# A four-layer graph network on one core: seven-product gates and one operation list that treats the SBUF way shared by VectorE and GpSimd as held by one engine at a time

## Chip, cores, metric

One NeuronCore of a Trainium2 chip; everything is fp32. The metric is the device time of one execution in microseconds.

## The reference, cut to what matters

128 graphs of 64 nodes with 256 features go through four residual layers, each behind a layer norm and a relu. Two graphs share the 128 partitions, and four such pairs form a group, so there are 16 groups of 512 nodes.

```python
h = relu(layernorm(x)); x = x + gat(h, adj, ...)      # layer 0: attention, 4 heads of 64
h = relu(layernorm(x)); x = x + gat(h, adj, ...)      # layer 1: attention, 1 head of 256
h = relu(layernorm(x)); x = x + relational(h, ...)    # layer 2: with 0/1 edges only its loop direction counts
h = relu(layernorm(x))                                # layer 3: gated recurrence, 3 steps
for i in range(3):
    m = h @ weight[i]; aggr = A.T @ m
    gi = aggr @ w_ih.T + b_ih; gh = h @ w_hh.T + b_hh
    r = sigmoid(i_r + h_r); z = sigmoid(i_z + h_z); n = tanh(i_n + r * h_n)
    h = (1 - z) * n + z * h
x = x + h
```

## The kernel before

Three stages stand one behind the other: attention (two groups alternating, layer 0 of one beside layer 1 of the one before), the relational layer, the recurrence. The recurrence of one step, with features on partitions (`c` is the half of the features, a `gate` is four matmuls of 512 columns for r and z and two for each part of n):

```python
into, own = (wc[:, i], aT), (whh, hT)
hnew = work.tile([P, K, T], F32, name="hT")
for c in range(K):
    pr = gate("rz", c, (own, into))
    ph = gate("nn", 4 + c, (own,))
    pi = gate("nn", 4 + c, (into,))
    pz = gate("rz", 2 + c, (own, into))
    nc.scalar.activation(r, pr, AF.Sigmoid, bias=brz[:, c : c + 1])
    nc.vector.scalar_tensor_tensor(t, ph, bh[:, 4 + c : 5 + c], r, op0=ALU.add, op1=ALU.mult)
    nc.vector.tensor_tensor(t, t, pi, ALU.add)
    nc.scalar.activation(nt, t, AF.Tanh, bias=bi[:, 4 + c : 5 + c])
    nc.scalar.activation(z, pz, AF.Sigmoid, bias=brz[:, 2 + c : 3 + c])
    nc.gpsimd.tensor_tensor(d, hT[:, c, :], nt, ALU.subtract)
    nc.gpsimd.tensor_tensor(d, d, z, ALU.mult)
    nc.vector.tensor_tensor(hnew[:, c, :], nt, d, ALU.add)
# ... cut: hnew back to nodes on partitions by 8 transposes
```

## Time and profile before

| | before |
|---|---|
| time, median of the first 3 runs | 2235.72 us (2230.89 to 2236.61) |
| TensorE busy, granted clock | 83%, 0.879 |
| VectorE / ScalarE / GpSimd busy | 46% / 20% / 19% |

Busy shares are averages over stages with different limits, so the prediction reads the span in slices and stretches. It shows those lines.

### The profile page before, as it was taken

What the parts mean: (1) busy time and instruction counts of PE and PEld (TensorE: products, weight loads), DVE (VectorE), ACT (ScalarE), POOL (GpSimd) and SP (SyncE); (2) the same over time, 40 slices, a digit from 0 to 9 for tenths busy, and PEclk for the clock granted to TensorE, in tenths of its full rate; (3) what the DMA queues carried; (4) which work ended last, traced back from release to release, by engine and by line L of the source; (5) the groups of instructions that cost most, each with busy time, mean ns of one, the idle gap of its engine ahead of it and who ended that gap; (6) DMA issues with size and microseconds to landing.
All of it is one profiled execution on the core that took longest, in us unless ns stands there. A gap on an engine that the chain in (4) does not pass through costs nothing.

```text
span 2234.7 us, 16784 instructions
## 1 busy us (share of the span) xinstructions
PE 1865.9 (83%) x6149; PEld 1072.5 (48%) x6149; DVE 1019.7 (46%) x2244; ACT 442.4 (20%) x708; POOL 432.6 (19%) x364
## 2 busy tenths in 40 slices
PE   3857675766666668887999999999999999999998
PEld 2545454555455434444444544544444454444444
DVE  4576767676767554433433323332333233333222
ACT  1122222122222112222111111121112111111111
POOL 1111221122112210000222122222212212121221
PEclk8876666666666579998999999999999999999999
DMA  8000000000000000000000000000000000000000
GB/s 230 29 1 0 1 0 0 1 1 0 0 0 1 0 2 0 1 0 0 1 10 10 10 0 10 10 10 0 10 10 10 0 10 10 10 3 8 10 10 10
DMA packets 31592, 23.95 MB, mean 11 GB/s; under 512 B 11280, under 2 KB 31504, under 8 KB 31504
## 3 DMA queue, kind: packets, MB, share of 16 engines
q1 hardware_dynamic: 25344, 18.88, 2.7%
q10 hardware_dynamic: 6160, 3.94, 0.6%
q8 instruction: 50, 0.82, 0.1%
q14 instruction: 38, 0.31, 0.0%
HBM read 14.43 MB, written 8.39 MB: 10 GB/s over the span
## 4 chain that ended last, share of the span: by engine, by line
PE 73%; DVE 15%; ACT 6%; POOL 4%; issue 2%; DMA 1%; POOLq 0%; ACTq 0%; DVEq 0%
PE rz L535 27%; PE nn L535 14%; PE mm L289 6%; PE mm L468 5%; PE mm L228 4%; PE tp L524 4%; PE tp L284 3%; POOL d L556 3%; PE tp L154 2%; PE ht L568 2%; PE mm L491 2%; PE pe L248 2%; DVE em L301 2%; DVE var L143 2%; ACT eb L273 2%
## 5 line engine op out<-in xcount | busy, mean ns | idle before, releaser
L535 PE MATMUL rz<-hT,whh 128*128 128x512 f32 x768 | 378.1, 596 | 4.7 <-ACT hT L155 4.7
L535 PE MATMUL rz<-aT,wc 128*128 128x512 f32 x768 | 366.1, 599 | 0.0
L555 POOL TENSOR_TENSOR d<-hT,nt 128x512 f32<-128x512 f32 x96 | 121.5, 1266 | 740.8 <-ACT nt L551 740.8
L557 DVE TENSOR_TENSOR hT<-nt,d 128x512 f32<-128x512 f32 x96 | 66.4, 692 | 434.5 <-POOL d L556 434.5
L535 PEld LDWEIGHTS rz<-aT,wc 128*128 128x128 f32 x768 | 139.6, 190 | 173.1 <-issue 144.7
L535 PEld LDWEIGHTS rz<-hT,whh 128*128 128x128 f32 x768 | 138.3, 191 | 142.7 <-issue 134.5
L535 PE MATMUL nn<-hT,whh 128*128 128x512 f32 x384 | 185.7, 592 | 0.0
L284 PE MATMUL tp<-ident,eb 128*128 128x128 f32 x320 | 80.8, 416 | 121.4 <-ACT eb L273 121.4
L535 PE MATMUL nn<-aT,wc 128*128 128x512 f32 x384 | 180.4, 592 | 0.0
L546 ACT ACTIVATE r<-rz,brz 128x512 f32<-128x512 f32 x96 | 66.0, 687 | 517.9 <-PE rz L535 517.9
L289 PE MATMUL mm<-wh,ec 128*128 128x65 f32 (+1 forms) x640 | 160.9, 423 | 3.8 <-DVE ec L285 2.4
L548 DVE SCALAR_TENSOR_TENSOR t<-nn,bh,r 128x512 f32<-128x512 f32 x96 | 72.0, 750 | 201.0 <-PE nn L535 172.1
L154 PE MATMUL tp<-ident,hn 128*128 128x128 f32 x512 | 94.6, 337 | 75.6 <-DVE hn L147 70.5
L289 PEld LDWEIGHTS mm<-wh,ec 128*128 128x128 f32 x640 | 136.8, 302 | 26.6 <-DVE ec L285 18.3
L556 POOL TENSOR_TENSOR d<-d,z 128x512 f32<-128x512 f32 x96 | 121.4, 1264 | 105.6 <-ACT z L553 105.6
L468 PE MATMUL mm<-hT,wl 128*128 128x512 f32 x256 | 120.5, 614 | 17.6 <-ACT sg L473 13.8
L155 ACT ACTIVATE hT<-tp 128x512 f32<-128x512 f32 x128 | 71.2, 594 | 299.2 <-PE tp L154 289.6
L284 PEld LDWEIGHTS tp<-ident,eb 128*128 128x128 f32 x320 | 65.5, 236 | 129.3 <-ACT eb L273 129.3
L228 PE MATMUL mm<-w0e,hT 128*128 128x264 f32 x256 | 81.0, 454 | 55.6 <-DVE es L233 54.6
L551 ACT ACTIVATE nt<-t,bi 128x512 f32<-128x512 f32 x96 | 69.3, 721 | 279.2 <-DVE t L549 279.2
L154 PEld LDWEIGHTS tp<-ident,hn 128*128 128x128 f32 x512 | 78.2, 175 | 94.9 <-DVE hn L147 82.2
L535 PEld LDWEIGHTS nn<-aT,wc 128*128 128x128 f32 x384 | 73.0, 190 | 91.8 <-issue 91.8
(95 smaller groups left out, 2210.0 us busy)
## 6 DMA issues: line engine op xcount, KB each, us to landing
X<-in_x_dram SPq DMA_DIRECT2D x16, 512.0 KB, 6.5
out_dram<-hnat SPq DMA_DIRECT2D x16, 512.0 KB, 2.9
A<-in_adj_dram SPq DMA_DIRECT2D x16, 128.0 KB, 6.0
ihn<-in_L_gnn_w_ih_dram ACTq DMA_DIRECT2D x1, 768.0 KB, 10.8
wn<-in_L_gnn_weight_dram ACTq DMA_DIRECT2D x3, 256.0 KB, 2.6
ihn<-in_L_gnn_w_hh_dram ACTq DMA_DIRECT2D x1, 768.0 KB, 4.8
w0e<-in_L_gnn_W_dram ACTq DMA_DIRECT2D x1, 256.0 KB, 4.4
w1e<-in_L_gnn_W_dram ACTq DMA_DIRECT2D x1, 256.0 KB, 5.8
```

Of the source, the lines that this page charges most:

```text
L154: nc.tensor.transpose(pt[:, p * P : (p + 1) * P], hn[:, p, k * P : (k + 1) * P], ident)
L155: nc.scalar.activation(hT[:, k, :], pt, AF.Relu)
L228: nc.tensor.matmul(pm[:, : D + 2 * heads], hT[:, k, p * P : (p + 1) * P], we[:, k, :], start=(k == 0), stop=(k == K - 1),)
L284: nc.tensor.transpose(pt[:, h * P : (h + 1) * P], eb[:, first + h, :], ident)
L289: nc.tensor.matmul(pv[:, h, :], ec[:, p * heads + h - first, :], wv[:, p, h, :], start=True, stop=True)
L468: nc.tensor.matmul(pm, wl[:, k, col : col + P], hT[:, k, :], start=(k == 0), stop=(k == K - 1))
L524: nc.tensor.matmul(pa[:, p * P : (p + 1) * P], hnat[:, p, c * P : (c + 1) * P], abd[:, p, :], start=True, stop=True,)
L535: nc.tensor.matmul(pg, l, r, start=(j == 0), stop=(j == len(ops) - 1))
L548: nc.vector.scalar_tensor_tensor(t, ph, bh[:, 4 + c : 5 + c], r, op0=ALU.add, op1=ALU.mult)
L551: nc.scalar.activation(nt, t, AF.Tanh, bias=bi[:, 4 + c : 5 + c])
L555: nc.gpsimd.tensor_tensor(d, hT[:, c, :], nt, ALU.subtract)
L556: nc.gpsimd.tensor_tensor(d, d, z, ALU.mult)
```

## The change

The intent: fewer columns through TensorE for the r and z gates, no stage that leaves TensorE waiting, and an order of each engine's instructions that is worked out in advance. The program is first recorded as operations with their dependencies, a duration, and a deadline by group and layer. A list maker then issues them to the engines' queues by an own clock: of what could start earliest, the one due first.

The 1696 lines of the diff come to four pieces. First the clock, with the shared way: the access to SBUF that VectorE and GpSimd cannot use at the same time (the prediction shows it in a trace). `port` is how long an operation needs it:

```diff
+            t, _, op, places = best          # key = (start, due), over all engines
+                # ... cut: the operation is issued; DMA queue apart
+                took = op.cost
+                if op.port:
+                    other = "Pool" if e == "DVE" else "DVE"
+                    took = max(took, held[other] + min(op.port, took) - t)
+                    held[e] = t + took
+# ... cut
+def port(engine, method, writes, reads):
+    if method not in ("tensor_tensor", "scalar_tensor_tensor", "tensor_scalar", "tensor_copy"):
+        return 0.0
+    n = elements(writes[0])
+    reads = [v for v in reads if elements(v) >= n]
+    if engine == "gpsimd":
+        return 50.0 + 2.1 * n if n >= 64 else 0.0
+    if engine != "vector" or any(v.base.pool.psum for v in [*writes, *reads]):
+        return 0.0
+    return 15.0 + n * (1.04 if len(reads) > 1 else 0.53)
```

Then the seven products. The halves of the nodes `S0`, `S1`, the halves of the features and the two gates r and z make a product of two 2x2 block matrices; sums of the blocks (`ws` of weights, `ms` of states, made on GpSimd) let seven products of 256 columns do for eight. The partial results are read from PSUM by copies and additions in between:

```diff
-                    pr = gate("rz", c, (own, into))
-                    pz = gate("rz", 2 + c, (own, into))
+                # ... cut: one product is a pair of weights and states, chosen by its number
+                    1: (w[:, 0, cs], m[:, 0, S0]),
+                    2: (w[:, 1, cs], m[:, 1, S0]),
+                    3: (ws[:, 2, cs], m[:, 1, S1]),
+                    4: (w[:, 1, zs], ms[:, 3]),
+                    5: (ws[:, 0, cs], ms[:, 0]),
+                    6: (ws[:, 1, cs], ms[:, 1]),
+                    7: (w[:, 0, zs], ms[:, 2]),
```

Third, attention builds its weights as min(max(t·g, f), mask) of exponentials, with sources on the free axis: no transposes of the weights, no maximum to subtract. Fourth, sigmoids become tanh of half the argument, and the features are fetched per group instead of staying on chip. The general relational path moved behind a flag test at the end and does not run on this data.

The deadlines are constants of the program, in us: `start, period = 100, 91.8`, times of the layers for the first three groups, and for later groups `end - 70 * i` with `end = start + g * period - 49`.

## The prediction

> **What bounds the kernel now.** I read the page's table by engine and its 40 slices first, then busy time in four stretches cut where the stages change, then the chain of waits inside two of them, then the groups by line.
>
> ```profile
> PE   3857675766666668887999999999999999999998
> DVE  4576767676767554433433323332333233333222
> PEclk8876666666666579998999999999999999999999
> ```
>
> Two kernels stand one behind the other here. In the first half neither TensorE nor VectorE is full and the granted clock is at 0.6 to 0.7. In the second half TensorE is full at full clock while VectorE falls to a third. The stretches give numbers:
>
> ```profile
> core 0: us, PE busy (x) PEld busy (x) DVE busy (x) ACT busy (x) POOL busy (x), PEclk, DMA share, GB/s
> 0.00:55.00 55.00, 17.17 (x44) 10.56 (x45) 25.00 (x71) 5.96 (x9) 8.29 (x13) 0.89 0.83 234
> 55.00:850.00 795.00, 532.47 (x1985) 400.13 (x1985) 520.53 (x1241) 168.13 (x296) 155.30 (x132) 0.69 0.01 3
> 850.00:1085.00 235.00, 191.50 (x638) 104.93 (x637) 98.90 (x276) 55.54 (x91) 20.14 (x20) 0.95 0.00 0
> 1085.00:2234.00 1149.00, 1124.76 (x3488) 556.92 (x3487) 375.31 (x656) 212.76 (x312) 248.91 (x199) 1.00 0.02 8
> ```
>
> Attention (55 to about 805 us) is bound by a chain that passes from engine to engine; the recurrence (from 1054 us) is bound by TensorE. The chain in each:
>
> ```profile
> 424.33 1.24 DVE t L253
> 425.58 1.22 DVE t L259
> 426.81 0.33 DVE t L253
> 427.14 1.25 DVE t L262
> ```
> ```profile
> 1505.15 6.01 PE rz L535 x14
> 1511.15 3.43 PE nn L535 x8
> ```
>
> In attention the end hangs on VectorE steps of 1.2 us in a row, with TensorE standing. In the recurrence it is matmul after matmul: 14 passes in 6.01 us, 429 ns each. So the GRU stage can only become shorter by fewer columns through TensorE, and the attention stage only by putting it beside something else.
>
> **The columns, before.** An fp32 matmul is two passes in this trace, a transpose one. Start to start of neighbours in the trace: 429 ns at 512 columns, 222 at 264, 217 at 258, 216 at 256, 109 to 112 at 128 and 112 at 65 (the fastest tenth at full clock). By the counts of the groups by line: r and z gates 1536 x 0.429 = 659 us; n gates 768 x 0.429 = 329; values of the two attention layers 256 x 0.222 + 256 x 0.217 = 112; loop weights 256 x 0.429 = 110; everything else (transposes, 65-column aggregates, adjacency products, weights) 401. Sum **1611 us**, of a span of 2235. The other 624 us are idle time and half clock, nearly all before 1085 us.
>
> **What the Trainium skill says.** "TensorE: Matmul & The Clock Gate", Part 1: after an idle window of about 3.4 us the array's clock falls to half, and sustained work brings it back. This trace agrees: 0.69 in attention, 1.00 in the recurrence. "Perfetto Trace Analysis", Optimization Strategy: where the most contended engine changes over time, interleave those regimes; this trace is such a case, and this is what the change does. "SBUF — State Buffer", Who interferes with whom: VectorE in a two-port mode, or with two SBUF inputs, and a GpSimd operation that reads SBUF exclude each other for the whole instruction. The trace agrees at least for the one-input kind:
>
> ```profile
> 409.74 2.34 POOL L304 TENSOR_TENSOR X<-X,em 128x1024 f32<-128x1024 f32 x1 [3.20 <-DVE em L303]
> ```
> ```profile
> 409.85 2.25 DVE L143 TENSOR_SCALAR var<-mv 128x4 f32<-128x4 f32 x1
> ```
>
> A VectorE operation on four elements, 170 ns at the median, takes 2.25 us and ends as GpSimd's addition ends. The two-input kind never meets GpSimd in this kernel, so no run shows it yet. "ScalarE: Activation LUTs", Table sets: exp and tanh are in one set. Before loads tables four times (1.28 us each); after replaces sigmoid by tanh of half the argument and has one load. Worth 4 us, no more.
>
> **Part 1, seven products instead of eight.** For r and z the two halves of the features, the two gates and the two halves of the nodes make a 2x2 by 2x2 product. It is done with seven products of 256 columns where eight halves stood. The order of the changed kernel has 1344 such matmuls: 2688 passes x 0.216 = 581 us against 659. Saved on TensorE: **78 us**. Added: four sums per state or aggregate, 384 on GpSimd, each 185 + 2.11 x 256 = 725 ns (the line through its 1266 ns at 512 and 2347 ns at 1024 elements); one copy on ScalarE and one addition on VectorE for three of the four half gates.
>
> **Part 2, attention without its matrices turned.** The weights are built with sources already on the free axis, so the 320 transposes of eb (35 us), most of the pe products (34 us) and 128 transposes of vT (14 us) go; small transposes and the early groups' products come in (11 us). Saved: **72 us**. The subtraction of the maximum, the predicated copy and the reduction per head on VectorE go as well. New is a way through DRAM for one row per group and head, which has tens of us to land in, as it is listed a period ahead.
>
> The TensorE floor after: 581 + 329 + 112 + 110 + 329 for everything else = **1461 us**.
>
> **Part 3, one list for everything.** Group g's recurrence runs beside the attention and loop layers of later groups, each engine's order fixed in advance with durations that match this trace (427 ns a pass, 682 ns for a 512-element VectorE operation, 1275 for GpSimd). So the 624 us should shrink to: a head, a tail, and what TensorE still waits.
> Head: the first matmul started at 23.1 us here, behind the input; the first groups' layers are one dependent chain, and by 55 us TensorE had done 17 us of work. Halving the first groups helps a little. I take 45 us of idle.
> Tail: the last recurrence has no filler left. Its three layers wait for a chain of aT copy (0.59), three sums on GpSimd (2.2) and, at the end, addition, tanh, two VectorE steps on a half (0.4 each): about 5 us a layer, 15 us, plus output (2.9 us to land). I take 20 us.
> Middle: the old recurrence kept TensorE busy 1124.76 of 1149 us, 98%, with coarse pieces. Now TensorE has 1611 waits listed (1484 before) in pieces of half the size, with fuller engines beside it. I choose **95%**: 1461 / 0.95 = 1538.
> Sum: 45 + 20 + 1538 = 1603, say **1600 us**, a ratio of 0.716.
>
> **The other engines, by the same rows.** VectorE: layernorms 227 us (unchanged); recurrence 192 x 5 + 96 = 1056 operations on 256 elements at 0.40 (the busy time per instruction of o) = 420; attention about 300, loop 100, the rest 55. Sum 1100 us, 69% of 1600. ScalarE: 288 copies at 0.37, 576 tanh at 0.415 (the 64x256 row), 96 biases at 0.69, 160 copies of 512 at 0.59, and the layers' own, about 735 us, 46%. GpSimd: 576 x 0.725 = 418, powers 70 x 1.01 = 71, additions to x 28 x 2.35 = 66, others 20: 575 us, 36%. The shared way: GpSimd's 555 us of reading plus VectorE's two-input and two-port operations (recurrence 576 x 0.41 = 236, attention 171, others about 75) make some 1040 us held, 65%. It fits. Unplanned, about 1000 such VectorE operations would meet GpSimd with chance 555/1600 and lose some 0.45 us: 160 us, which brings VectorE to 79%. The list counts this, so I expect less.
>
> **The rivals.**
> 1. VectorE with the shared way becomes the bound. If every microsecond of GpSimd blocked VectorE: 1100 + 555 = 1655, with head and tail about 1720. For it: 2.25 us for four elements, as shown, and nearly every new VectorE operation of the recurrence has two SBUF inputs. Against: VectorE reads PSUM or one input in a good half of its time, and the order is made for this.
> 2. The recurrence's own chain becomes the bound. 48 layers in 1500 us leave 31 us each; TensorE's own work in one is (581 + 329 + 85 + 42) / 48 = 21.6 us, so about 10 us of filler must land in the right gaps. If the chain needs 34 us a layer: 48 x 34 + 100 before the first = 1730. For it: seven products add copies and sums to the chain, and a fixed order cannot swap in what is ready. Against: the old chain of gate, tanh and state cost 2.9 us per layer and was hidden to 98%.
> 3. The list holds almost exactly: 98% and a head and tail of 55 us give 1491 + 55 = 1546. For it: the period written into the plan, 91.8 us, is 3% over 1461 less the 29 us of setup, by 16 groups (89.5). I do not take more from that number than intent.
> 4. The clock does not come up, because short waits still leave idle windows. At 0.9 instead of 1.0, 1461 becomes 1623 and the total about 1760. Against: the recurrence held 1.00 over 1149 us, and even at 81% busy (850 to 1085 us) the clock was 0.95.
>
> **Range and chances.** Rival 3 sets the lower end, 1550; a middle of 91% with head and tail of 70 us sets the upper, 1461 / 0.91 + 70 = 1675, which I draw in to 1665, since rivals 1 and 2 each have perhaps one chance in ten. Slower than before by 2% would need 2280 us, hundreds above the worst rival; only the general branch being taken, which the data's 0/1 edges exclude, could do it. Faster 0.98, same 0.01, slower 0.01.
>
> **What would show it.** In the profile after: TensorE at full clock and 9 in nearly every slice from about 60 us on; its busy share over 90%; matmul steps of 216 ns in the ry, rm and rz products; VectorE between 65% and 80%, and GpSimd near 36%, evenly over the span; the chain that ended last mostly TensorE. Step 1 is wrong if the 256-column passes follow each other at more than 230 ns (weight loads no longer hidden). Step 3 is wrong if a stretch in the middle shows TensorE under 90%; the waits of TensorE then name the rival: VectorE operations of z, d or hT lasting far over 0.41 us for rival 1, sums on GpSimd or aT on ScalarE for rival 2, a clock under 0.97 for rival 4. The whole is wrong if the span is under 1530 or over 1700.

## The result

| | before | after |
|---|---|---|
| time, median of 4 runs each | 2233.3 us | 1551.68 us (1549.9 to 1553.41) |
| ratio | | 0.6947 (0.6933 to 0.6961) |
| TensorE busy, granted clock | 83%, 0.879 | 96%, 0.988 |
| VectorE / ScalarE / GpSimd busy, us | 1020 / 442 / 433 | 1152 / 717 / 641 |

Predicted were 1600 us and a range of 1550 to 1665. The result lies just inside its lower end.

The same three rows of the page as before, 40 slices of the changed kernel's span:

```profile
PE   5979999999999999999999999999999999999997
DVE  6778786968688686878868697886969778666444
PEclk8979999999999999999999999999999999999999
```

The two regimes of before are gone. From the fourth slice to the last but one TensorE is at 9 at full clock, and VectorE is at 6 to 9 until the last three slices, where it is at 4. The dip in the third slice belongs to the head of the program. In stretches (busy time of each engine, granted clock, DMA share, GB/s):

```profile
core 0: us, PE busy (x) PEld busy (x) DVE busy (x) ACT busy (x) POOL busy (x), PEclk, DMA share, GB/s
0.00:60.00 60.00, 40.12 (x168) 29.03 (x169) 39.70 (x122) 20.12 (x57) 20.43 (x37) 0.91 0.47 132
60.00:120.00 60.00, 50.33 (x205) 33.85 (x203) 43.91 (x139) 21.15 (x57) 16.34 (x25) 0.83 0.04 10
120.00:1400.00 1280.00, 1267.04 (x5878) 944.50 (x5877) 993.13 (x2543) 609.89 (x1388) 555.08 (x620) 1.00 0.07 20
```

In the changed kernel every operation passes through one recording helper, so all lines are L370 and the tiles tell the groups apart: `hn` normalised features, `eb` attention weights, `aT` aggregate, `hT` state, `aS` and `hS` their sums, `r` and `z` gates, `t` candidate, `d` difference of state and candidate. TensorE's longest waits there (who waited, for whom, us in total, times, longest):

```profile
PE tp L370 <- DVE hn L370: 14.3, 1, 14.3
PE rm L370 <- DVE hT L370: 8.8, 13, 0.9
PE tp L370 <- DVE var L370: 6.1, 1, 6.1
PE mm L370 <- DVE eb L370: 5.0, 5, 2.3
```

14.3 us are the wait for the first input and 6.1 us a single wait at 101 us; the wait that repeats most is for the state `hT`, as a next step's first products start.

**Where the 682 us went.** Passes start one after another at 429 ns for 512 columns, 216 for 256 and 109 to 112 for 128 in the changed kernel too, seven products included. So I can weigh all passes at those times, as the prediction did ("floor"), and call the rest of a stretch lost:

| | floor | lost |
|---|---|---|
| before, whole span 2234.7 | 1611 | 623 |
| after, whole span 1551.6 | 1461 | 91 |
| after, 0 to 120 us | 71.8 | 48.2 |
| after, 120 to 1400 us | 1253.5 | 26.5 |
| after, 1400 to 1551.6 us | 135.6 | 16.0 |

By this account 150 us of the gain are fewer columns, 532 us are time that TensorE no longer loses to waits and half clock.

**The shared way.** GpSimd's and VectorE's timelines of the changed kernel at 631 us (start, duration):

```profile
631.19 2.35 POOL L370 TENSOR_TENSOR xg<-xg,hn 128x1024 f32<-128x1024 f32 x1 [3.81 <-DVE hn L370]
```
```profile
632.02 1.80 DVE L370 SCALAR_TENSOR_TENSOR t<-r,t 128x256 f32<-128x256 f32 x1 [0.39 <-ACT r L370]
```

An operation with two SBUF inputs that takes 0.42 us alone begins inside GpSimd's addition, takes 1.80 us and ends 0.28 us after it. The groups by line show who suffers (count, busy us, mean ns of one):

```profile
L370 DVE SCALAR_TENSOR_TENSOR t<-r,t 128x256 f32<-128x256 f32 x192 | 128.6, 675 | 97.6 <-ACT r L370 74.6 <-ACT t L370 21.1
L370 DVE SCALAR_TENSOR_TENSOR hT<-d,t 128x256 f32<-128x256 f32 x192 | 102.8, 553 | 2.4
L370 DVE SCALAR_TENSOR_TENSOR d<-z,d 128x256 f32<-128x256 f32 x192 | 100.7, 536 | 38.1 <-POOL d L370 22.6 <-ACT z L370 14.9
L370 DVE TENSOR_TENSOR z<-rz,z 128x256 f32<-128x256 f32 x192 | 80.4, 419 | 68.5 <-PE rz L370 57.5 <-ACT z L370 10.1
```

The same number of elements four times: `z` has one input in PSUM and takes 419 ns whether GpSimd works or not (418 and 419 ns in the trace); `t`, `hT` and `d` have both in SBUF and take 416 to 418 ns without GpSimd beside them, and 960, 717 and 661 ns on average with it. Over all VectorE operations I count about 155 us lost so, and 71 us on GpSimd (time beyond each form's undisturbed duration).

### The profile page after: what moved, and what is told of

Its sections match the earlier page's. It is cut to its first block, busy times and chain, and to the rows that moved or that the text cites. A ratio compares the mean times of both kernels' runs of the same rounds, so it can differ in the third digit from the quotient of the medians.

```text
span 1551.6 us, 20462 instructions
## 1 busy us (share of the span) xinstructions
PE 1496.4 (96%) x6837; PEld 1106.9 (71%) x6837; DVE 1152.0 (74%) x2971; ACT 716.9 (46%) x1645; POOL 641.1 (41%) x748
## 4 chain that ended last, share of the span: by engine, by line
PE 79%; DVE 12%; POOL 4%; issue 2%; ACT 2%; DMA 1%; ACTq 0%; SPq 0%; DVEq 0%
PE mm L370 20%; PE ry L370 18%; PE nh L370 10%; PE tp L370 9%; PE ni L370 8%; PE rz L370 8%; PE rm L370 5%; DVE hT L370 3%; POOL aS L370 2%; DVE d L370 2%; DVE hn L370 2%; DVE t L370 2%; POOL hS L370 1%; DVE eb L370 1%; POOL d L370 1%
## 5 line engine op out<-in xcount | busy, mean ns | idle before, releaser
L370 POOL TENSOR_TENSOR d<-hT,t 128x256 f32<-128x256 f32 x192 | 149.7, 790 | 460.8 <-ACT t L370 459.5
L370 DVE SCALAR_TENSOR_TENSOR t<-r,t 128x256 f32<-128x256 f32 x192 | 128.6, 675 | 97.6 <-ACT r L370 74.6
L370 PE MATMUL nh<-hT,whh 128*128 128x512 f32 x384 | 195.4, 597 | 1.8 <-DVE hT L370 1.8
L370 PE MATMUL ni<-aT,wc 128*128 128x512 f32 x384 | 194.3, 594 | 0.0
L370 ACT ACTIVATE z<-z,brz 128x256 f32<-128x256 f32 x192 | 97.1, 506 | 75.2 <-DVE z L370 75.0
L370 DVE TENSOR_TENSOR z<-rz,z 128x256 f32<-128x256 f32 x192 | 80.4, 419 | 68.5 <-PE rz L370 57.5
L370 DVE SCALAR_TENSOR_TENSOR d<-z,d 128x256 f32<-128x256 f32 x192 | 100.7, 536 | 38.1 <-POOL d L370 22.6
L370 POOL TENSOR_TENSOR hS<-hT 128x256 f32<-128x256 f32 x96 | 81.1, 849 | 105.1 <-PE ry L370 94.8
L370 PE MATMUL mm<-wl,hT 128*128 128x512 f32 x248 | 121.0, 598 | 0.0
L370 ACT COPY z<-ry 128x256 f32<-128x256 f32 x192 | 71.0, 370 | 107.7 <-PE ry L370 88.3
L370 POOL TENSOR_TENSOR aS<-aT 128x256 f32<-128x256 f32 x96 | 92.2, 961 | 58.8 <-ACT aT L370 58.8
L370 DVE TENSOR_SCALAR hn<-xg,mv,rstd 128x256 f32<-128x256 f32 x256 | 115.1, 491 | 1.4 <-POOL rstd L370 1.2
L370 PE MATMUL ry<-hS,wsum 128*128 128x256 f32 x384 | 115.3, 382 | 0.4 <-ACT z L370 0.4
L370 PE MATMUL rz<-hS,whh 128*128 128x256 f32 x384 | 114.9, 381 | 0.5 <-DVE z L370 0.5
L370 PE MATMUL ry<-aS,wsum 128*128 128x256 f32 x384 | 114.3, 379 | 0.0
L370 PE MATMUL rz<-aS,wc 128*128 128x256 f32 x384 | 114.2, 379 | 0.0
L370 POOL TENSOR_TENSOR rstd<-var,mhalf 128x4 f32<-128x4 f32 (+1 forms) x70 | 74.5, 1069 | 95.2 <-DVE var L370 93.8
L370 PE MATMUL tp<-abd,hnat 128*128 128x128 f32 x768 | 108.6, 276 | 0.0
L370 PEld LDWEIGHTS tp<-abd,hnat 128*128 128x128 f32 x768 | 103.0, 192 | 5.9 <-issue 1.4
L370 PEld LDWEIGHTS ry<-hS,wsum 128*128 128x128 f32 x384 | 69.6, 190 | 51.7 <-issue 24.3
L370 PE MATMUL tp<-ident,hn 128*128 128x128 f32 x512 | 85.7, 278 | 20.9 <-DVE hn L370 14.3
L370 POOL TENSOR_TENSOR aS<-aT,aS 128x256 f32<-128x256 f32 x96 | 88.7, 925 | 41.5 <-ACT aT L370 40.7
```

The lines of the kernel that those rows point to most:

```text
L370: return do(*[real(a) for a in args], **{k: real(v) for k, v in kwargs.items()})
```

## The experiments

Twelve kernels ran, all correct. Times are medians; "lost" is as above. Comparisons go over ratios to the kernel before, as the chips differ: its median was 2230 to 2236 us throughout.

| run | us | ratio | TensorE's share at floor, 120 to 1400 us |
|---|---|---|---|
| after | 1551.7 | 0.6947 | 97.9% |
| e1 shared way not counted | 1636.9 | 0.7334 | 91.4% |
| e2 eight products | 1601.3 | 0.7176 | 99.5% |
| e3 program order | 3137.0 | one look | 47.9% |
| e4 more columns | 1616.5 | 0.7246 | 99.4% |
| e5 longer, not exclusive | 1590.9 | 0.7118 | 95.3% |
| e6 eight products, sums kept | 1606.1 | 0.7184 | 99.2% |
| e7 other deadlines | 1525.6 | 0.6825 | 99.4% |
| e8 those, way not counted | 1565.9 | 0.7003 | 96.4% |
| e9 eight products, e7's deadlines | 1598.8 | 0.7160 | 99.8% |
| e10 more columns, e7's deadlines | 1609.1 | 0.7207 | 99.4% |
| e11 subtraction on VectorE | 1519.7 | 0.6805 | 99.4% |
| e12 order by deadline | 2669.1 | one look | 53.2% |

### e1: the shared way not counted

```diff
 def port(engine, method, writes, reads):
+    return 0.0
```

> Only the list changes: its clock no longer holds VectorE back while GpSimd has the shared way, or the other way round. The instructions are the same, so TensorE's floor stays 1461 us. Theory (the counting is worth time, because a listed order cannot swap in what is ready): VectorE's two-input operations on 256 elements (t, d, hT) lengthen beyond the 675, 536 and 553 ns of the changed kernel, TensorE falls from 98% to 95% or 96% between 200 and 1400 us, and the span is 1580 to 1620 us. Rival (VectorE at 74% has slack enough, the semaphores absorb it): span within 0.7% of 1552 us, 1541 to 1562, whatever the operations last.

1636.86 us, ratio 0.7334: 85 us more than the changed kernel for the same instructions in another order. The direction is the theory's, beyond its numbers. But its means of getting there failed. The groups by line of e1:

```profile
L370 DVE SCALAR_TENSOR_TENSOR hT<-d,t 128x256 f32<-128x256 f32 x192 | 109.5, 582 | 4.1
L370 DVE SCALAR_TENSOR_TENSOR t<-r,t 128x256 f32<-128x256 f32 x192 | 104.8, 546 | 88.7 <-ACT r L370 68.9 <-ACT t L370 19.1
L370 DVE SCALAR_TENSOR_TENSOR d<-z,d 128x256 f32<-128x256 f32 x192 | 99.5, 530 | 39.6 <-POOL d L370 24.1 <-ACT z L370 15.1
```

`t` is shorter than in the changed kernel (546 against 675 ns), `hT` a little longer, `d` the same. Over all of VectorE about 138 us are lost to the way, against 155. The list that counts the way does not avoid collisions; VectorE loses a little more time in them. What it does is expect them. TensorE's longest waits in e1:

```profile
PE tp L370 <- DVE hT L370: 20.7, 16, 2.6
PE tp L370 <- DVE hn L370: 14.2, 1, 14.2
PE mm L370 <- ACT aT L370: 12.7, 13, 1.1
PE tp L370 <- DVE var L370: 6.7, 2, 6.3
PE ry L370 <- ACT z L370: 6.5, 14, 0.5
PE mm L370 <- DVE o L370: 6.2, 23, 0.7
```

In place of one repeated wait there are many, on VectorE and on ScalarE. I read them so: the list placed matmuls at moments at which their operands would have been ready, had VectorE not been held, and as the order is fixed, nothing else could be taken in their place. The waits fit this reading; they do not prove it, and e5 and e8 test it further.

### e2: eight products

The chunk's products 1 to 7, their copies and additions and all sums are replaced by:

```diff
+            def prod(self, name, k, source):
+                w, m = ((whh, self.hT), (wc[:, self.i], aT))[source]
+                f = {"rm": 0, "rz": D}[name] + self.c * P
+                ps, new = self.bank(name)
+                nc.tensor.matmul(ps, w[:, k, f : f + P], m[:, k, :], start=new, stop=(source == 1 and k == 1))
```

> The r and z gates as before, eight half products (768 matmuls of 512 columns), without the sums of weights and states, the copies and the additions; the freed PSUM bank goes to the shared pool. Same list maker. Theory (TensorE's columns bind): floor 1461 + 78 = 1539 us and about the same 90 us lost, so 1620 to 1640 us. Rival (what the seven products add on GpSimd, 384 sums of about 0.87 us, on ScalarE, 288 copies, and on VectorE, 288 additions, costs time too, so taking it away gives part back): 1575 to 1610 us.

1601.34 us, ratio 0.7176: 50 us more than with seven products, where TensorE's floor grows by 78 (1461 to 1539). The rival's range held, though not its reason, as e6 and e9 show. The 28 us between them lie mostly in the middle of the span: eight products lost 6.6 us from 120 to 1400 us, seven 26.5. What eats them stays open here; e6, e7 and e9 take it up.

### e3 and e12: the same operations in plainer orders

e3 takes operations as the program states them, e12 by deadline, both without the clock:

```diff
-                        key = (t, op.due)
+                        key = (op.number, 0)          # e3;  (op.due, op.number) in e12
```

> Same operations, but each engine's list is the order in which the program states them, group after group, without any look at time. Theory (the list's interleaving, not the cheaper attention, makes most of the gain): a group's three layers (a chain of some 85 us) and its recurrence (69 us of columns and its own waits) follow each other, 16 x 150 to 190 us = 2400 to 3000 us, TensorE clock under 0.8. Rival (fewer operations and columns do most, and engines that run ahead through their queues do the rest): under 1800 us.

> Same operations and same deadlines as the changed kernel, but the list takes, of all operations whose inputs are listed, the one due first; it has no clock and does not ask when an engine is free or an operand there. Theory (interleaving by deadlines alone is not enough; each engine must be given what will be ready when it is free): 2100 to 2500 us, between e3 and the changed kernel. Rival (any interleaved order fills TensorE): under 1750 us.

3137.03 and 2669.14 us, one look each, both slower than the kernel before and beyond the top of the range expected, with the cheaper attention and the seven products in place. The page of e3, then that of e12:

```profile
PE   5584664847557375574746648466583755738466
PEclk8696786968869587786967868678696876958778
```
```profile
PE   6654657777777668767776776767667676867776
PEclk8775778888888889868798888789888878879888
```

TensorE is at 3 to 8 with the clock at 0.5 to 0.9 from end to end. Even an order that interleaves groups by deadline (e12) leaves it waiting: its longest wait, 262.5 us in all, is for VectorE's `hT` before the state is transposed, and the fixed order lets nothing be taken in between.

### e4: more columns for TensorE alone

```diff
+                if name == "nh" and new:
+                    nc.tensor.matmul(ps, w[:, k, f : f + P], m[:, k, :], start=True, stop=True)
                 nc.tensor.matmul(ps, w[:, k, f : f + P], m[:, k, :], start=new, stop=not new)
```

> The first matmul of each nh gate is issued twice (the second begins the sum anew, so the result is the same): 96 x 2 passes of 429 ns = 82 us more on TensorE and nothing on any other engine. Theory (TensorE binds over nearly the whole span): 1552 + 82 = 1634 us, at least 1620. Rival (another engine or the chain of the recurrence binds, and TensorE has room): below 1585 us.

1616.5 us, ratio 0.7246: 65 us for 82 us of columns. That is near the theory, but short of its least number by 3.5 us. In the middle TensorE loses 8 us now, not 26.5: the added columns took the place of some waits, or the list, made anew for them, came out better. So the changed kernel is bound by TensorE up to some 20 us in the middle, and those can be had (e7).

### e5: longer operations, not exclusive ones

```diff
                 if op.port:
-                    other = "Pool" if e == "DVE" else "DVE"
-                    took = max(took, held[other] + min(op.port, took) - t)
-                    held[e] = t + took
+                    took += 135.0 if e == "DVE" else 100.0
```

> The list again does not hold the two engines apart; instead it takes every operation that needs the shared way as longer by a fixed amount, 135 ns on VectorE and 100 ns on GpSimd, which is about what such operations lost on average where the way was not counted (t, hT, d and hn took 546, 582, 530 and 541 ns instead of 407 to 418; the sums 756 to 902 instead of 726). Theory A (the list only has to know how much work VectorE and GpSimd have): 1550 to 1575 us. Theory B (it has to know which operation stands at which moment, because one order is fixed): 1590 to 1640 us.

1590.94 us, ratio 0.7118, on the lower edge of theory B's range. It gives back 46 of e1's 85 us. For these deadlines, telling the list the mean length did about half, and the moments would be the rest. But each figure is one list, and e8 shows that the cost of not counting differs by 45 us between two sets of deadlines, so the split is not settled.

### e6: eight products with the sums kept

```diff
                 along(psum, hnat, abd, aT, 0)
+                aS = work.tile([P, 4, T // 2], F32, name="aS")
+                state_sums(aT, aS, 0)                  # and the others alike; nothing reads them
```

> Eight half products, with the 384 sums on GpSimd put back though nothing reads them. The question is where 28 of the 78 us went that the seven products save on TensorE: with eight products TensorE lost only 7 us between 120 and 1400 us, with seven 26 us. Theory A (the sums cost it, by taking the shared way from VectorE): 1615 to 1630 us instead of 1601. Theory B (the dependencies of the seven products cost it: half gates that wait for copies, additions and sums before TensorE may use the bank again): 1598 to 1606 us, no change, though VectorE's operations become longer.

1606.13 us, ratio 0.7184 against e2's 0.7176: no change, at the upper edge of theory B. VectorE's operations do become longer. Groups of e2, then of e6:

```profile
L370 DVE SCALAR_TENSOR_TENSOR hT<-d,t 128x256 f32<-128x256 f32 x192 | 72.1, 414 | 0.1
```
```profile
L370 DVE SCALAR_TENSOR_TENSOR hT<-d,t 128x256 f32<-128x256 f32 x192 | 93.9, 528 | 0.1
```

414 to 528 ns, and in all VectorE loses about 150 us to the way instead of 67, for 5 us of time. So the sums' work and their collisions are not what cost the 28 us of e2. That leaves dependencies of the seven products or an order that fits them badly. One reserve: dead sums can wait for a convenient moment, which live ones can't.

### e7: other deadlines

```diff
-        start, period = 100, 91.8
+        start, period = 96.0, 91.8
-                end = start + g * period - 49
-                units = [(0, G, [end - 70 * i for i in (3, 2, 1, 0)])]
+                end = start + g * period - 47.1
+                units = [(0, G, [end - 48.2 * i for i in (3, 2, 1, 0)])]
```

(and a few of the first groups' deadlines, by up to 12 us.)

> Same program and same list maker with the shared way counted; only the deadlines handed to it differ (first recurrence due 4 us earlier, layers of the later groups 48 us apart instead of 70, their last one 2 us later, the first weights 2 us earlier). They were searched for with the list maker's own clock, which ends 20 us earlier. TensorE has 48 us of idle time before 120 us and 26 us from 120 to 1400 us to give back. If the list's clock is right as it was within 20 us for the changed kernel: 1530 to 1540 us. If the chip follows such small differences no more: 1545 to 1560 us.

1525.61 us, ratio 0.6825: 26 us under the changed kernel and 4 below the range. The stretches of e7:

```profile
60.00:120.00 60.00, 54.13 (x244) 38.13 (x243) 46.74 (x155) 23.55 (x68) 19.78 (x31) 0.97 0.04 10
120.00:1400.00 1280.00, 1278.80 (x5937) 956.37 (x5936) 971.95 (x2561) 614.38 (x1401) 524.65 (x621) 1.00 0.07 20
```

From 60 to 120 us the clock is 0.97 instead of 0.83 and TensorE is busy 4 us longer and does 8 us more of its passes, weighed as above; in the middle the floor fills 99.4% instead of 97.9%. With all seven products in place the 26.5 us are down to 8.

### e8: the same deadlines, the way not counted

```diff
 def port(engine, method, writes, reads):
+    return 0.0                                # on top of e7
```

> The deadlines of e7, with the shared way not counted as in e1. A control for chance: one list may be bad by luck. Theory (not counting is what cost 85 us in e1): 1600 to 1660 us, at least 60 us over e7. Rival (e1 was an unlucky list): within 25 us of e7.

1565.86 us, ratio 0.7003: 40 us over e7, between the rival's 25 and the theory's 60. Both were off. Not counting costs time under both sets of deadlines, 85 us in e1 and 40 here, so its cost depends on the list that comes out. From 120 to 1400 us TensorE's largest wait in e8 is for the gate `r` on ScalarE, 17.7 us in 13 waits, against 0.5 us in e7. One reserve: e7's deadlines were searched for with the clock that counts the way. No list without the counting was given deadlines of its own, so 40 us may still be too much. Here too VectorE loses less to the way (about 94 us) than where it is counted (121 in e7), and yet the kernel is slower.

### e9: eight products with e7's deadlines

> Eight half products with the deadlines of e7. What the seven products save is to be read between two lists that both fill TensorE (e7: 99.4% between 120 and 1400 us; e2: 99.5%). Theory A (nothing inherent ate the 28 us; the deadlines of the changed kernel fitted the seven products less well): at least 68 us over e7, 1593 to 1604 us. Theory B (the seven products need their own waits, and the deadlines only moved them): 1570 to 1585 us.

1598.83 us, ratio 0.7160: 73 us over e7 by the medians, 75 by the ratios. Theory A. Where both lists fill TensorE to 99% or more, seven products save about what their columns say: 73 of 78 us. So the 28 us of e2 came from the changed kernel's deadlines, which served eight products better than seven; e7's were searched for with seven, but eight have only 3 us left to gain in the middle under them.

### e10: more columns with e7's deadlines

> The 82 us of repeated first matmuls of e4, on top of e7. In e4 they cost 65 us, as 20 us of the changed kernel's idle time between 120 and 1400 us were filled by them. e7 has only 8 us left there. Theory (TensorE binds, and nearly all its idle time is head and tail): 75 to 82 us over e7, 1600 to 1608 us. Rival (the chain between engines binds too): 60 us or less over e7.

1609.06 us, ratio 0.7207: 83.5 us over e7 by the medians, 85 by the ratios, for 82 us of columns, a microsecond or two over the expected range. Here the time follows TensorE's columns one for one.

### e11: the subtraction on VectorE

```diff
-                nc.gpsimd.tensor_tensor(self.d[:, h], self.hT[:, self.c, h], t, ALU.subtract)
+                nc.vector.tensor_tensor(self.d[:, h], self.hT[:, self.c, h], t, ALU.subtract)
```

(with deadlines searched anew.)

> The 192 subtractions h - n move from GpSimd (about 790 ns each) to VectorE (about 415 ns), with deadlines searched anew for it in the same way; the way stays counted. VectorE gets 79 us more work, GpSimd 150 us less, and less time is lost to the shared way. Theory (TensorE binds, the rest has room): 1516 to 1528 us, at most 10 us under e7's 1526. Rival 1 of the prediction (VectorE with the shared way is close to the bound): more than 1535 us, as VectorE is over 75% busy; or, if the waits for the way were it, under 1510.

1519.67 us, ratio 0.6805 (0.679 to 0.682), within the theory's range. VectorE is busy 77% of the span and the kernel is no slower. It is the fastest version here, though its gain over e7 (0.6803 to 0.6847) is within the intervals: the two were not run on one chip. Both beat the kernel before and the changed one clearly.

## Why the prediction was right, point by point

**The range: right, with luck.** 1551.68 us clears the lower end by 1.7 us. e7, the same program with other deadlines, took 1525.61 us, outside the range and under the 1530 us at which the prediction called itself wrong as a whole. What bounds the kernel was foreseen; that this list landed inside was not.

**What bounds, and the columns: right.** The floor of 1461 us came out to the microsecond, since the counts were read from the changed program and the steps held (216 ns for 256 columns, weight loads hidden).

**Part 1, seven products, 78 us: right in size, and only under fitting deadlines.** 50 us as shipped (e2), 73 us between lists that both fill TensorE (e9).

**Part 3, head 45 us, tail 20 us: near.** Measured 48 us up to 120 us and 12 us from 1500 us on.

**The middle at 95%: the mis-sized term.** The prediction allowed 77 us of loss for it (1538 less 1461). From 120 to 1500 us the chip lost 30, that is 97.8%. This one term, 47 us too large, makes nearly the whole distance from 1600 to 1552; the tail was 8 us too large and the head 3 too small. The old recurrence's 98% was the better guide; that more waits and half-size pieces would cost 3% more was a guess, and e7 fills 99.4% from 120 to 1400 us with the same pieces. (The prediction's 1611 and 1484 waits stand in no view; the two traces record 1933 and 1565 TensorE instructions with a wait, so there are more, as it says.)

**"The list counts this, so I expect less" than 160 us lost to the shared way: wrong.** About 155 us were lost on VectorE, and uncounted lists lose less (138 in e1, 94 in e8). Counting was worth 40 to 85 us with deadlines made for a list that counts; that the list then places TensorE's work by when operands really come is the likeliest reason, read from the waits and from e5.

**The other engines.** ScalarE came to 717 us against 735. GpSimd took 641 instead of 575, the difference being the 71 us for which the way was held against it, which the prediction had not set down for GpSimd. VectorE's 1152 us seem to fit between the 1100 unblocked and the 1260 blocked, but that is two errors against each other: without the 155 us lost its own work was about 997 us, some 100 less than predicted, and the loss was as large as the one estimated for an unplanned order.

**The rivals.** Rival 1 (VectorE with the way binds) did not come true: VectorE was at 74%, e6 loses 83 us more to the way than e2 for 5 us of time, e11 fills VectorE to 77%. Rival 2 (the recurrence's chain) left a trace: the repeated wait for `hT`, 8.8 us in all. Rival 4 (clock) showed only at the ends: 0.83 from 60 to 120 us and 0.94 from 1500 us on. The prediction says that the trace agrees with the page on the clock; it does so in the two levels, but not in the idle window of 3.4 us (see the last section). Rival 3 (the list holds almost exactly, 98%, head and tail 55 us, 1546 us in all) is what happened (97.8%, 60 us, 1552), and it deserved more weight than the lower end of the range.

**What I cannot settle.** Why the changed kernel's deadlines leave seven products 26 us of loss in the middle, and which single deadline of e7 mends it, was not taken apart.

## What to carry to other kernels

When every engine's order is fixed, do not expect a contention model to make the contention smaller (155 us with it, 138 without): judge it by the waits of the engine that binds. Weigh that engine's work at its measured steps first; here that floor plus head and tail was the answer within 2%, and fill-in work between dependent steps did more (532 us) than fewer columns (150 us). Before a cleverer algorithm is called disappointing, give both versions an order that suits each; for the counting of the way itself that was not done here.

## What the Trainium skill lacked or had wrong

- "SBUF — State Buffer", Who interferes with whom: the rule held as stated, also for two SBUF inputs, which the kernel before could not show (0.42 us became 1.80 us beside a GpSimd addition of 2.35 us; with one input in PSUM 419 ns either way). The section lists `tensor_scalar` through its two-port mode alone. Here the normalisation `hn`, a `tensor_scalar` with two per-partition scalars, took 408 ns for 256 elements, no faster than a one-input-in-PSUM operation of that size, and was still held: 545 ns on average beside GpSimd. No run shows why.
- The same page, Summary: rules for kernel authors, says to "Schedule whichever is off the critical path". No page says what the blocking costs a fixed order: 40 us (e8 against e7) to 85 us (e1) of some 1550 if the order ignores it, and nearly nothing (5 us for 83 us of blocking, e6 against e2) if it counts it and there is room.
- "TensorE: Matmul & The Clock Gate", Part 1: the granted clock took only the two levels that the page names, full and half. But the page ties the fall to an idle window of about 3.4 us, and of the 40 falls in the kernel before, 24 had no gap of TensorE over 2.7 us in the 10 us ahead of them (matmul ends are modelled); the fall at 868.6 us came after 3.4 us in which TensorE was busy for 1.7.
- "Perfetto Trace Analysis", Optimization Strategy: it says that interleaving regimes may help, not that the interleaving must follow readiness. The same operations took 1552 us in a clocked order, 2669 us interleaved by deadline and 3137 us in program order, where the kernel before took 2234.
